# Second pass of a quantised feed-forward in written order, one PSUM bank per chunk; all keys in the first pass

## The chip, the cores and the metric

The kernel runs on one core of one Trainium2 chip. A core has a matrix engine (TensorE, PE in the profile; its weight loads are listed as PEld), a vector engine (VectorE, DVE), a scalar engine (ScalarE, ACT), a general engine (GpSimd, POOL) and a synchronising engine that issues transfers (SyncE, SP). Each engine works through its own instruction queue in order and waits there on semaphores that the others raise. Matrix products land in PSUM, which the kernel uses as eight banks of 2 KB a partition; a bank holds 512 fp32 values a partition. The metric is the time on the device in microseconds (us) of one execution of the whole program, lower is better.

## The reference, cut to what matters

Two transformer layers on an activation `x` of 16 x 256 x 256, each with a cross attention and a feed-forward. The change lies in the feed-forward of layer 0, which is quantised, and in what lies beside it: pieces of layer 1's attention that depend on the context alone.

```python
def quant_act_uint8(x):                       # one scale for the whole tensor
    s = max(max(x), EPS) / 255.0
    return clip(round(x / s), 0, 255) * s, s
def quant_linear(x, w, b):                    # weights int8 by channel, bias int32
    xq, s_in = quant_act_uint8(x)
    return einsum('btd,fd->btf', xq, wq) + bq
h = relu(quant_linear(layernorm(x), w1, b1))  # 256 -> 1024
x = x + quant_linear(h, w2, b2)               # 1024 -> 256
# layer 1 attention: correlation by delays of queries and keys, averaged over
# heads, channels and batch; the best 6 delays; softmax; values rolled by them
corr = irfft(rfft(q) * conj(rfft(k)))
index = top_k(corr.mean(...), 6)
```

The scale of `h` is a maximum over all of `h`, so no value of `h` can be quantised before the largest is known.

## The kernel before

The 4096 rows of `x` stay in SBUF as 32 tiles of 128 rows (`NT`), taken in 8 blocks (`NB`) of 4 tiles (`TB`), 512 rows each. The hidden width of 1024 is 8 chunks (`FC`) of 128, the model width of 256 is 2 (`DC`). A framework with tile pools builds the instruction streams: it puts in the semaphore waits, and where the code does not say otherwise, a scheduler chooses the order of instructions on each engine. Inside a `manual_schedule` region PE's instructions stand in the order in which the code writes them.

**First pass** (`first`, L914, and the loop from L1007). For each block, `integers_of` (L982) makes the block's integers: per tile one activation into a buffer `u` on ACT, two DVE operations, then 8 bf16 transposes into `qT`. For each pair of chunks, four matmuls (two chunks of two matmuls, 512 columns) fill a tile `ph` of two banks, and DVE reduces it to a maximum (`hmax`, L1013). PE's order is written out here. In the gaps stand keys of layer 1: `keys1` (L924) loads the context of one batch row (`ck`, on SP), turns it with four transposes, ACT writes `cT`, eight matmuls make `pk` and ACT writes `gT`. Four of the 16 keys are made ahead of the pass, ten in it, and the last two behind it in the scheduler's order.

**Max chain** (L1029 to L1051): DVE reduces `hmax`, POOL takes the maximum over partitions (`all_max`, L867), DVE works out the scale and the factors `a1`, `c1` of the next activation.

**Second pass** (loop at L1104 to L1112, scheduler's order). `hidden` (L1053) makes the same products again, a pair of chunks in a two-bank tile of the pool `ps_h` (two such tiles), ACT turns each chunk into `h32` (relu with scale and bias, L1060), DVE rounds it into `hq` (L1068). `second` (L1070) multiplies `hq` with the second weights (`py`, 16 matmuls a block), ACT writes `yT` (L1083), 8 transposes (`ytp`) turn it, DVE adds it to `x` (L1097) and takes the statistics of the next layer norm (`ln_stats`, L97), and once a block `ln_rstd` (L102) makes `rstd2` with eleven small DVE operations. The pools are `ps_h` (2 x 2 banks), `ps_b` (2) and `ps_y` (2): all eight banks.

**Start of layer 1's attention** (L1168 on, the x2 stage). `values1` (L957) is a product of context and value weights for one batch row, six matmuls on PE and a copy on ACT; it depends on nothing of layer 0 and fills PE where something is waited for. Three of them stand ahead of this stage. For each block, `ln_apply` (L118) makes normalised rows `xn`, eight transposes make `x2tp`, DVE and ACT copy them into `q`, and two groups of eight matmuls make `pm` (L1192) against `gT`; each `pm` goes through DRAM and comes back skewed (`skew`), and `diagonals` (L1142) adds them up in `pr`. Then `pmean` (L1248), with two `values1` ahead of the last diagonals and the rest, seven, behind `pmean`, while DVE and ACT find the best delays (L1254 to L1281), `cd` is written to DRAM and SP brings it back as `cm` (L1303); `po` (L1307) needs `cm`. Behind that stand the gates and a mixture of experts, which is most of the time.

Of the kernel before, what the change touches and what calls it, by code (L numbers as in the profile page):

```python
# [8 lines left out]
F32 = mybir.dt.float32  # L9
# [9 lines left out]
P = 128  # L19
# [9 lines left out]
def tile_kernel(ctx: ExitStack, tc: tile.TileContext, io: dict, out: bass.AP):  # L29
# [67 lines left out]
    def ln_stats(mv, t):  # L97
        st = small.tile([P, 6], F32, tag="bn", name=f"bn_{t}")
        nc.vector.bn_stats(st, x[:, t, :])
        nc.vector.bn_aggr(mv[:, t, :], st)  # L100

    def ln_rstd(rstd, mv, t0, n, who, by=1.0):  # L102

        ve = small.tile([P, n], F32, tag="ve", name=f"ve_{who}_{t0}")
        nc.vector.tensor_scalar(ve, mv[:, t0 : t0 + n, 1], LN_EPS, None, ALU.add)
        first = small.tile([P, n], I32, tag="r0", name=f"r0_{who}_{t0}")
        nc.vector.tensor_scalar(first, ve.bitcast(I32), -0.5, float(0x5F3759DF), ALU.mult, ALU.add)
        y = first.bitcast(F32)
# [771 lines left out]
    gq = until_keys.enter_context(tc.tile_pool(name="gq", bufs=1, side="right"))  # L880
    gT = gq.tile([P, B, DC, S], F32, name="gT")
    with tc.tile_pool(name="pb", bufs=2) as pb, tc.tile_pool(
        name="ps_h", bufs=2, space=PSUM
    ) as ps_h, tc.tile_pool(name="ps_b", bufs=2, space=PSUM) as ps_b, tc.tile_pool(
        name="ps_y", bufs=2, space=PSUM
    ) as ps_y:
        ln_rstd(rstd1, mv1, 0, NT, "1")
        g0 = sc.tile([P, NT], F32, name="g0")
        nc.vector.tensor_tensor(g0, rmax1, mv1[:, :, 0], ALU.subtract)
# [21 lines left out]
        qT = pb.tile([P, DC, NT * P], BF16, tag="qT", bufs=1, name="qT")  # L911
        hmax = sc.tile([P, FC, NB], F32, name="hmax")

        def first(blk, ph, fc):  # L914
            for c in range(DC):
                nc.tensor.matmul(  # L916
                    ph,
                    w1T[:, c, fc * P : (fc + 1) * P],
                    qT[:, c, blk * 512 : (blk + 1) * 512],
                    start=(c == 0),  # L920
                    stop=(c == DC - 1),
                )

        def keys1(b, pool=None, tag="y"):  # L924

# [77 lines left out]
        with tc.manual_schedule(engines={mybir.EngineType.PE}):  # L1003
            for _ in integers_of(0):
                pass
            key = None
            for blk in range(NB):  # L1007
                ahead = integers_of(blk + 1) if blk + 1 < NB else iter(())
                for f0 in range(0, FC, 2):
                    ph = ps_h.tile([P, 2, 512], F32, tag="h", name=f"ph1_{blk}_{f0}")  # L1010
                    for f in range(2):
                        first(blk, ph[:, f, :], f0 + f)
                    nc.vector.tensor_reduce(  # L1013
                        hmax[:, f0 : f0 + 2, blk], ph, axis=AX.X, op=ALU.max
                    )
                    if f0 < 4:
                        next(ahead, None)
                    if key is not None:
                        next(key)
                        key = None  # L1020
                    elif f0 == 2 or (f0 == 6 and blk % 4 == 0):
                        key = keys1(next(keyed))
                        next(key)
        for b in keyed:
            for _ in keys1(b):
                pass


        m1 = sc.tile([P, FC], F32, name="m1")  # L1029
# [20 lines left out]
        nc.vector.tensor_scalar(bq2, bq2, MAGIC, MAGIC, ALU.add, ALU.subtract)  # L1050
        nc.vector.tensor_mul(bq2, bq2, s2)  # L1051

        def hidden(blk, hq, f0):  # L1053

            ph = ps_h.tile([P, 2, 512], F32, tag="h", name=f"ph2_{blk}_{f0}")
            for f in range(2):
                fc = f0 + f
                first(blk, ph[:, f, :], fc)
                h32 = pb.tile([P, 512], F32, tag="h32", bufs=4, name=f"h32_{blk}_{fc}")
                nc.scalar.activation(  # L1060
                    h32,
                    ph[:, f, :],
                    AF.Relu,
                    bias=c1[:, fc : fc + 1],
                    scale=a1[:, fc : fc + 1],
                )

                nc.vector.tensor_scalar(hq[:, fc, :], h32, MAGIC, MAGIC, ALU.add, ALU.subtract)  # L1068

        def second(blk, hq):  # L1070

            yT = pb.tile([P, DC, 512], F32, tag="yT", name=f"yT{blk}")
            for c in range(DC):
                py = ps_y.tile([P, 512], F32, tag="y", name=f"py{blk}_{c}")
                for fc in range(FC):
                    nc.tensor.matmul(
                        py,
                        w2T[:, fc, c * P : (c + 1) * P],
                        hq[:, fc, :],
                        start=(fc == 0),  # L1080
                        stop=(fc == FC - 1),
                    )
                nc.scalar.activation(  # L1083
                    yT[:, c, :], py, AF.Identity, bias=bq2[:, c : c + 1], scale=s2[:, c : c + 1]
                )
                yield
            for i0 in range(0, TB, 2):
                t = blk * TB + i0
                tp = ps_b.tile([P, 2, D], F32, tag="b", name=f"ytp{blk}_{i0}")
                for i in range(2):  # L1090
                    for c in range(DC):
                        nc.tensor.transpose(
                            tp[:, i, c * P : (c + 1) * P],
                            yT[:, c, (i0 + i) * P : (i0 + i + 1) * P],
                            ident,
                        )
                nc.vector.tensor_tensor(x[:, t : t + 2, :], tp, x[:, t : t + 2, :], ALU.add)  # L1097
                for i in range(2):
                    ln_stats(mv2, t + i)
                if i0 + 2 == TB:  # L1100
                    ln_rstd(rstd2, mv2, blk * TB, TB, "2")
                yield

        pend = None  # L1104
        for blk in range(NB + 1):
            hq = pb.tile([P, FC, 512], BF16, tag="hq", name=f"hq{blk}") if blk < NB else None
            for f0 in range(0, FC, 2):
# [698 lines left out]
```

## Time and profile before

Times of three runs: 1407.86 us median, 1406.86 to 1409.86.

| what | value |
|---|---|
| profiled execution, its own time | 1407.56 us |
| its span, first to last instruction | 1405.9 us |
| mean granted clock of PE | 0.995 of full speed |
| PE busy in the span | 1358.8 us, 97% |
| DVE, ACT, POOL busy | 633.8, 553.3, 239.0 us |
| second pass, first relu to the last hq | 500.2 to 573.2 us |
| first `pm` of layer 1 | 581.70 us |

A row of the timeline gives the start, the busy time, the engine, the line of the kernel, the operation, what it writes and reads with the shapes, and how many in a row; in brackets the idle time before it and what ended it. Matmuls overlap, so the distance between two starts says more than the time of one.

### The profile page before, as it was taken

The page shows a single profiled execution, that of the slowest core. Times are in us where ns is not written, and L with a number is a line of the kernel's source. Part 1 is how long each engine was busy: PE and PEld are TensorE (multiplying, and loading weights), DVE is VectorE, ACT ScalarE, POOL GpSimd, SP SyncE. Part 2 cuts the span into 40 slices and gives each one's busy share as a digit, 9 for nine tenths or more (in the row PEclk, how much of TensorE's full clock was granted, in tenths as well). Part 3 has the DMA queues.
Part 4 walks back from the last instruction along what each step waited for, and adds up shares of the span by engine and source line. Part 5 has one row for each costly group of instructions (what it writes and reads, how often), then busy time and mean ns, then how long its engine had stood idle before and what let it go on. Part 6 is the DMA issues. An engine that isn't in the chain of part 4 may idle for free. (4 is left out here: it accounts for less than half of the span.)

```text
span 1405.9 us, 24030 instructions
## 1 busy us (share of the span) xinstructions
PE 1358.8 (97%) x8881; PEld 1035.8 (74%) x8955; DVE 633.8 (45%) x2520; ACT 553.3 (39%) x1050; POOL 239.0 (17%) x312
## 2 busy tenths in 40 slices
PE   6999999999989999999999999999999999999998
PEld 3565655666647644678788888888888888888887
DVE  7688879887737868857830101011011110101025
ACT  1454545554447568423622222323322323222221
POOL 6232133122000000000026530111111111111110
PEclk9899999999999999999999999999999999999999
DMA  9231323221001100333002245767666767665246
GB/s 276 78 96 54 105 85 91 70 73 27 17 18 37 45 0 1 112 98 96 3 31 83 72 156 195 249 231 244 244 248 233 246 236 257 234 232 190 96 155 220
DMA packets 127831, 184.06 MB, mean 131 GB/s; under 512 B 11600, under 2 KB 104952, under 8 KB 127712
## 3 DMA queue, kind: packets, MB, share of 16 engines
q1 hardware_dynamic: 117600, 152.55, 33.6%
q0 software_dynamic: 10112, 29.94, 6.1%
q8 instruction: 72, 1.18, 0.3%
q14 instruction: 47, 0.39, 0.1%
HBM read 141.16 MB, written 34.48 MB: 125 GB/s over the span
## 5 line engine op out<-in xcount | busy, mean ns | idle before, releaser
L1415 ACT ACTIVATE hTr<-pfr,bsel 128x256 f32<-128x256 f32 (+1 forms) x344 | 147.6, 430 | 345.9 <-PE pfr L1407 337.1
L1653 PE MATMUL ppr<-wp,hTr 128*128 128x256 f32 x1088 | 248.5, 379 | 0.0
L1407 PE MATMUL pfr<-xjT,wf 128*128 128x256 f32 (+1 forms) x1376 | 246.6, 338 | 0.7 <-DVE xjT L1643 0.7
L1407 PEld LDWEIGHTS pfr<-xjT,wf 128*128 128x128 f32 x1376 | 215.8, 191 | 30.3 <-issue 9.9
L1661 DVE TENSOR_TENSOR yj<-ppr,bj 128x512 f32<-128x512 f32 (+1 forms) x43 | 24.9, 580 | 440.3 <-PE ppr L1653 440.3
L1653 PEld LDWEIGHTS ppr<-wp,hTr 128*128 128x128 f32 x1088 | 202.1, 190 | 25.0
L511 DVE CUSTOM_DVE_ANT_0 junk<-sp,mb 128x256 bf16<-128x256 f32 x512 | 182.8, 420 | 37.6 <-PE sp L500 37.3
L588 ACT ACTIVATE pT<-st 128x1024 f32<-128x1024 f32 x128 | 124.4, 1021 | 125.9 <-PE st L578 125.9
L1679 POOL DMA_INDIRECT ys_d<-yj,to x68 | 65.4, 962 | 454.3 <-DVE to L1670 241.4
L1415 ACT ACTIVATE hTs<-pfs,bcol 128x256 f32<-128x256 f32 x128 | 59.9, 474 | 140.7 <-PE pfs L1407 137.5
L1407 PE MATMUL pfs<-xnT,wf-1_7251 128*128 128x256 f32 x512 | 114.5, 380 | 0.1
L1449 PE MATMUL pps<-wp-1_7253,hTs 128*128 128x256 f32 x496 | 109.6, 379 | 0.3 <-DVE x L1463 0.3
L1407 PEld LDWEIGHTS pfs<-xnT,wf-1_7251 128*128 128x128 f32 x512 | 96.4, 190 | 14.1 <-issue 1.4
L1449 PEld LDWEIGHTS pps<-wp-1_7253,hTs 128*128 128x128 f32 x496 | 94.2, 190 | 13.5 <-DVE x L1463 0.7
L500 PE MATMUL sp<-kT,qT 16*128 16x256 f32 x1024 | 93.4, 422 | 2.3 <-DVE mx L511 2.0
L568 PE MATMUL st<-qT,kT 32*128 32x256 f32 x1024 | 78.6, 404 | 0.7 <-DVE qT L549 0.7
L500 PEld LDWEIGHTS sp<-kT,qT 16*128 16x128 f32 x1024 | 59.2, 193 | 25.3 <-DVE mx L511 8.4
L1580 POOL DMA_INDIRECT xs_d<-xn,slot_i x64 | 61.8, 966 | 89.4 <-ACT hTs L1415 46.3
L601 PE MATMUL o<-pT,cxp 128*32 128x256 f32 x1024 | 73.6, 397 | 1.3 <-ACT pT L588 1.3
L916 PE MATMUL ph<-qT,w1T 128*128 128x512 bf16 x245 | 68.4, 378 | 4.0 <-DVE hmax L1013 1.4
L1463 DVE TENSOR_TENSOR x<-pps,x 128x512 f32<-128x512 f32 x15 | 10.4, 690 | 124.8 <-PE pps L1449 124.8
L568 PEld LDWEIGHTS st<-qT,kT 32*128 32x128 f32 x1024 | 50.7, 186 | 18.2 <-issue 12.4
(308 smaller groups left out, 1626.3 us busy)
## 6 DMA issues: line engine op xcount, KB each, us to landing
wf<-in_L_ffn_Wfc_dram SPq DMA_DIRECT2D x43, 1024.0 KB
wp<-in_L_ffn_Wproj_dram SPq DMA_DIRECT2D x43, 1024.0 KB, 5.7
xs_d<-zero POOLq DMA_DIRECT2D x36, 258.0 KB
yg<-ys_d SPq DMA_DIRECT2D x16, 512.0 KB, 6.4
xj<-xs_d SPq DMA_DIRECT2D x25, 258.0 KB
bj<-in_L_ffn_bproj_dram SPq DMA_DIRECT2D x43, 128.0 KB, 9.7
x<-in_x_dram SPq DMA_DIRECT2D x16, 256.0 KB, 10.7
cx<-in_ctx_dram SPq DMA_DIRECT2D x16, 256.0 KB, 2.7
```

The lines of the kernel that those rows point to most:

```text
L500: nc.tensor.matmul(sps[j // 2][:, j % 2, g, :], pr["qT"][rows, 2 * gp + g, qt * P : (qt + 1) * P], pr["kT"][rows, 2 * gp + g, :], start=Tr ...
L511: order["last"] = done = nc.vector.tensor_tensor_reduce(out=junk, in0=sps[j // 2][:, j % 2, g, :], in1=pr["mb"][:, qt, :], scale=1.0, scal ...
L568: nc.tensor.matmul(tps[j // 2][:, j % 2, k, :], pr["kT"][rows, g, k * P : (k + 1) * P], pr["qT"][rows, g, :], start=(k == 0), stop=False, ...
L588: nc.scalar.activation(pT, tps[i], AF.Exp)
L601: nc.tensor.matmul(pr["o"][HP * j : HP * (j + 1), g % 2, :], pr["cxp"][:, k, 4 * g + j, :], pTs[j // 2][:, j % 2, k, :], start=(k == 0), s ...
L916: nc.tensor.matmul(ph, w1T[:, c, fc * P : (fc + 1) * P], qT[:, c, blk * 512 : (blk + 1) * 512], start=(c == 0), stop=(c == DC - 1),)
L1407: nc.tensor.matmul(ph, wf[:, c, fc * P : (fc + 1) * P], rhs[:, c, :], start=(c == 0), stop=(c == DC - 1),)
L1415: nc.scalar.activation(hT[:, fc, :n], ph, AF.Gelu_apprx_tanh, bias=bias[:, fc : fc + 1]).ins
L1449: last = nc.tensor.matmul(po[:, i, :], hT[:, fc, i * P : (i + 1) * P], wp[:, fc, :], start=(fc == 0), stop=(fc == FC - 1),).ins
L1580: ins = nc.gpsimd.indirect_dma_start(out=xs_d, out_offset=bass.IndirectOffsetOnAxis(ap=slot_i[:, k, t : t + 1], axis=0), in_=xn3[t // QT][ ...
L1653: nc.tensor.matmul(po[:, i, :], hT[:, fc, i * P : (i + 1) * P], wp[:, fc, :], start=(fc == 0), stop=(fc == FC - 1),)
L1679: nc.gpsimd.indirect_dma_start(out=ys_d, out_offset=bass.IndirectOffsetOnAxis(ap=to[:, i : i + 1], axis=0), in_=yj[:, i, :], in_offset=None,)
```

## The change

Five things change together, all around the feed-forward of layer 0.

- The pools: `ps_y` and `ps_b` come first, `ps_h` is closed after the first pass, and its four banks become a pool `ps_k` of four tiles of one bank.
- The first pass: a key is begun in every second block at the last pair as well (before: in every fourth), so that all twelve keys are in the pass. Buffers of `u` go from 4 to 3. One `values1` follows the pass.
- The second pass is in written order on PE: per chunk its two first matmuls, two second matmuls of the block before, and one transpose of the block before that. Each chunk has a bank and a relu of its own; `first` names the previous relu as a dependency that takes part in the ordering alone and puts in no semaphore. A `values1` stands after chunk 3 of block 0 and another after the last second matmul.
- `rstd2` is made for blocks 0 to 3 together at block 3, for 4 to 6 at block 6, and for block 7 in the x2 stage; block 0's normalised rows (`xn_first`) are made at block 5.
- The x2 stage: one `values1` ahead of it instead of three, six instead of seven behind `pmean`; `ps_c` takes its banks after `ps_d` and `ps_r`.

```diff
     with tc.tile_pool(name="pb", bufs=2) as pb, tc.tile_pool(
-        name="ps_h", bufs=2, space=PSUM
-    ) as ps_h, tc.tile_pool(name="ps_b", bufs=2, space=PSUM) as ps_b, tc.tile_pool(
         name="ps_y", bufs=2, space=PSUM
-    ) as ps_y:
+    ) as ps_y, tc.tile_pool(name="ps_b", bufs=2, space=PSUM) as ps_b, ExitStack() as first_pass:
+        ps_h = first_pass.enter_context(tc.tile_pool(name="ps_h", bufs=2, space=PSUM))
...
-        def first(blk, ph, fc):
+        def first(blk, ph, fc, behind=None):
             for c in range(DC):
-                nc.tensor.matmul(
+                ins = nc.tensor.matmul(
...
+                if behind is not None and c == 0:
+                    tc.add_manual_dep(ins, behind.name, mybir.DependencyInfo(
+                            mybir.DependencyClass.NoSync, mybir.DependencyReason.DATA),
+                        reason="one chunk at a time")
...
-                u = pb.tile([P, D], F32, tag="u", bufs=4, name=f"u{t}")
+                u = pb.tile([P, D], F32, tag="u", bufs=3, name=f"u{t}")
...
-                    elif f0 == 2 or (f0 == 6 and blk % 4 == 0):
-                        key = keys1(next(keyed))
-                        next(key)
-        for b in keyed:
-            for _ in keys1(b):
-                pass
+                elif f0 == 2 or (f0 == 6 and blk % 2 == 0):
+                    key = keys1(next(keyed))
+                    next(key)
+        values1(next(valued), ps_b, "b")
+        first_pass.close()
+        ps_k = first_pass.enter_context(tc.tile_pool(name="ps_k", bufs=4, space=PSUM))
...
-        def hidden(blk, hq, f0):
-            ph = ps_h.tile([P, 2, 512], F32, tag="h", name=f"ph2_{blk}_{f0}")
-            for f in range(2):
-                fc = f0 + f
-                first(blk, ph[:, f, :], fc)
...
+        relus = []
+        def hidden(blk, hq, fc):
+            ph = ps_k.tile([P, 512], F32, tag="k", name=f"ph2_{blk}_{fc}")
+            first(blk, ph, fc, relus[-1] if relus else None)
+            h32 = pb.tile([P, 512], F32, tag="h32", bufs=4, name=f"h32_{blk}_{fc}")
+            relus.append(
                 nc.scalar.activation(
+                    h32, ph, AF.Relu, bias=c1[:, fc : fc + 1], scale=a1[:, fc : fc + 1]
+                ).ins
+            )
...
+                    if fc % 2 == 1:
+                        yield
...
-                if i0 + 2 == TB:
-                    ln_rstd(rstd2, mv2, blk * TB, TB, "2")
-                yield
+                            if i0 + 2 == TB and blk in (3, 6):
+                                b0 = 4 * (blk // 4)
+                                ln_rstd(rstd2, mv2, b0 * TB, (blk + 1 - b0) * TB, "2")
+                        yield
...
-        for blk in range(NB + 1):
-            hq = pb.tile([P, FC, 512], BF16, tag="hq", name=f"hq{blk}") if blk < NB else None
-            for f0 in range(0, FC, 2):
-                if blk < NB:
-                    hidden(blk, hq, f0)
-                if pend is not None:
-                    next(pend, None)
-            pend = second(blk, hq) if blk < NB else None
+        for blk in range(NB):
+            hq = pb.tile([P, FC, 512], BF16, tag="hq", name=f"hq{blk}")
+            for fc in range(FC):
+                hidden(blk, hq, fc)
+                next(mul, None)
+                next(turn, None)
+                if blk == 0 and fc == 3:
+                    values1(next(valued), ps_b, "b")
+            if blk == 5:
+                for i in range(TB):
+                    ln_apply(xn_first[:, i, :], mv2, rstd2, i)
+            turn = turned(blk - 1, yT) if blk > 0 else iter(())
+            yT = pb.tile([P, DC, 512], F32, tag="yT", name=f"yT{blk}")
+            mul = second(blk, hq, yT)
+        for _ in mul:
+            next(turn, None)
+        values1(next(valued), ps_b, "b")
+        for _ in turned(NB - 1, yT):
+            pass
...
-    ps_c = banks.enter_context(tc.tile_pool(name="ps_c", bufs=3, space=PSUM))
     ps_d = banks.enter_context(tc.tile_pool(name="ps_d", bufs=2, space=PSUM))
     ps_r = banks.enter_context(tc.tile_pool(name="ps_r", bufs=1, space=PSUM))
+    ps_c = banks.enter_context(tc.tile_pool(name="ps_c", bufs=3, space=PSUM))
...
-        for _ in range(3):
-            values1(next(valued), ps_c, "c")
+        values1(next(valued), ps_c, "c")
         for blk in range(NB):
-            xn = pc.tile([P, TB, D], F32, tag="xn", name=f"xn2_{blk}")
-            for i in range(TB):
-                ln_apply(xn[:, i, :], mv2, rstd2, blk * TB + i)
+            xn = xn_first
+            if blk > 0:
+                xn = pc.tile([P, TB, D], F32, tag="xn", name=f"xn2_{blk}")
+                for i in range(TB):
+                    ln_apply(xn[:, i, :], mv2, rstd2, blk * TB + i)
+            if blk == 1:
+                ln_rstd(rstd2, mv2, (NB - 1) * TB, TB, "2")
```

More of the change, by code (lines that the diff above doesn't have):

```diff
@@ L921, in first @@
                     stop=(c == DC - 1),
-                )
+                ).ins
+                if behind is not None and c == 0:
+                    tc.add_manual_dep(
+                        ins,
+                        behind.name,
+                        mybir.DependencyInfo(
+                            mybir.DependencyClass.NoSync, mybir.DependencyReason.DATA
+                        ),
+                        reason="one chunk at a time",
+                    )
         def keys1(b, pool=None, tag="y"):
@@ L999, in integers_of @@
                 yield
-        with tc.manual_schedule(engines={mybir.EngineType.PE}):
-            for _ in integers_of(0):
-                pass
-            key = None
-            for blk in range(NB):
-                ahead = integers_of(blk + 1) if blk + 1 < NB else iter(())
-                for f0 in range(0, FC, 2):
-                    ph = ps_h.tile([P, 2, 512], F32, tag="h", name=f"ph1_{blk}_{f0}")
-                    for f in range(2):
[L1012 to L1018, printed above, removed]
-                        next(key)
-                        key = None
-                    elif f0 == 2 or (f0 == 6 and blk % 4 == 0):
-                        key = keys1(next(keyed))
-                        next(key)
-        for b in keyed:
-            for _ in keys1(b):
-                pass
+        ordered = ExitStack()
+        ordered.enter_context(tc.manual_schedule(engines={mybir.EngineType.PE}))
+        for _ in integers_of(0):
+            pass
+        key = None
+        for blk in range(NB):
+            ahead = integers_of(blk + 1) if blk + 1 < NB else iter(())
+            for f0 in range(0, FC, 2):
+                ph = ps_h.tile([P, 2, 512], F32, tag="h", name=f"ph1_{blk}_{f0}")
+                for f in range(2):
+                    first(blk, ph[:, f, :], f0 + f)
+                nc.vector.tensor_reduce(
+                    hmax[:, f0 : f0 + 2, blk], ph, axis=AX.X, op=ALU.max
+                )
+                if f0 < 4:
+                    next(ahead, None)
+                if key is not None:
+                    next(key)
+                    key = None
+                elif f0 == 2 or (f0 == 6 and blk % 2 == 0):
+                    key = keys1(next(keyed))
+                    next(key)
+        values1(next(valued), ps_b, "b")
+        first_pass.close()
+        ps_k = first_pass.enter_context(tc.tile_pool(name="ps_k", bufs=4, space=PSUM))
         m1 = sc.tile([P, FC], F32, name="m1")
@@ L1051, in tile_kernel, with second @@
         nc.vector.tensor_mul(bq2, bq2, s2)
-        def hidden(blk, hq, f0):
-            ph = ps_h.tile([P, 2, 512], F32, tag="h", name=f"ph2_{blk}_{f0}")
-            for f in range(2):
-                fc = f0 + f
-                first(blk, ph[:, f, :], fc)
[L1059 to L1072, printed above, removed]
+        relus = []
[4 more added lines that the diff above has]
+            relus.append(
+                nc.scalar.activation(
+                    h32, ph, AF.Relu, bias=c1[:, fc : fc + 1], scale=a1[:, fc : fc + 1]
+                ).ins
+            )
+            nc.vector.tensor_scalar(hq[:, fc, :], h32, MAGIC, MAGIC, ALU.add, ALU.subtract)
+        def second(blk, hq, yT):
             for c in range(DC):
@@ L1082, in second, with turned @@
                     )
-                nc.scalar.activation(
-                    yT[:, c, :], py, AF.Identity, bias=bq2[:, c : c + 1], scale=s2[:, c : c + 1]
-                )
-                yield
+                    if fc == FC - 1:
+                        nc.scalar.activation(
+                            yT[:, c, :],
+                            py,
+                            AF.Identity,
+                            bias=bq2[:, c : c + 1],
+                            scale=s2[:, c : c + 1],
+                        )
+                    if fc % 2 == 1:
+                        yield
+        def turned(blk, yT):
             for i0 in range(0, TB, 2):
@@ L1096, in second @@
                         )
-                nc.vector.tensor_tensor(x[:, t : t + 2, :], tp, x[:, t : t + 2, :], ALU.add)
-                for i in range(2):
-                    ln_stats(mv2, t + i)
-                if i0 + 2 == TB:
-                    ln_rstd(rstd2, mv2, blk * TB, TB, "2")
-                yield
-        pend = None
-        for blk in range(NB + 1):
-            hq = pb.tile([P, FC, 512], BF16, tag="hq", name=f"hq{blk}") if blk < NB else None
-            for f0 in range(0, FC, 2):
-                if blk < NB:
-                    hidden(blk, hq, f0)
-                if pend is not None:
-                    next(pend, None)
-            pend = second(blk, hq) if blk < NB else None
+                        if i == 1 and c == DC - 1:
+                            nc.vector.tensor_tensor(
+                                x[:, t : t + 2, :], tp, x[:, t : t + 2, :], ALU.add
+                            )
+                            for j in range(2):
+                                ln_stats(mv2, t + j)
+                            if i0 + 2 == TB and blk in (3, 6):
+                                b0 = 4 * (blk // 4)
+                                ln_rstd(rstd2, mv2, b0 * TB, (blk + 1 - b0) * TB, "2")
+                        yield
+        mul, turn = iter(()), iter(())
+        xn_first = gq.tile([P, TB, D], F32, name="xn_first")
+        yT = None
+        for blk in range(NB):
+            hq = pb.tile([P, FC, 512], BF16, tag="hq", name=f"hq{blk}")
[15 more added lines that the diff above has]
+        for _ in turned(NB - 1, yT):
+            pass
+        ordered.close()
     sw = ctx.enter_context(tc.tile_pool(name="sw", bufs=1))
```

## The prediction

> **What bounds the kernel now.** I read the page's busy shares first, then the clock and the busy time of each engine by stage, then the start times inside the changed stage, then the chain behind the top-k. The page:
>
> ```profile
> span 1405.9 us, 24030 instructions
> PE 1358.8 (97%) x8881; PEld 1035.8 (74%) x8955; DVE 633.8 (45%) x2520; ACT 553.3 (39%) x1050; POOL 239.0 (17%) x312
> ```
>
> PE is the bound of the whole; a change pays only where PE stands idle. By stage (window, its length, PE, weight loads, DVE, ACT, POOL busy, granted clock, DMA share, GB/s):
>
> ```profile
> 440.00:502.00 62.00, 59.25 (x326) 38.87 (x333) 50.21 (x94) 39.01 (x111) 0.35 (x1) 1.00 0.13 39
> 502.00:573.00 71.00, 68.22 (x303) 30.11 (x307) 53.94 (x199) 55.76 (x79) 0.00 (x0) 1.00 0.00 1
> ```
>
> The first row is the first pass and the max chain, the second the second pass. Clock 1.00 in both. Busy PE is not PE at its peak: a lone matmul shows 0.38 us, but its successor can start earlier. The starts say what one costs. ScalarE (ACT) and PE in the second pass:
>
> ```profile
> 520.35 1.44 ACT L1060 ACTIVATE h<-ph,c,a 128x512 f32<-128x512 f32 x2
> ...
> 522.71 1.45 ACT L1060 ACTIVATE h<-ph,c,a 128x512 f32<-128x512 f32 x2 [0.24 <-PE ph L916]
> 524.83 1.45 ACT L1060 ACTIVATE h<-ph,c,a 128x512 f32<-128x512 f32 x2 [0.68 <-PE ph L916]
> 526.96 1.45 ACT L1060 ACTIVATE h<-ph,c,a 128x512 f32<-128x512 f32 x2 [0.68 <-PE ph L916]
> ...
> 529.34 1.44 ACT L1060 ACTIVATE h<-ph,c,a 128x512 f32<-128x512 f32 x2
> ```
> ```profile
> 568.94 0.38 PE L1076 MATMUL py<-hq,w2T 128*128 128x512 bf16 x1
> ...
> 569.61 1.46 PE L1076 MATMUL py<-hq,w2T 128*128 128x512 bf16 x6
> ...
> 574.72 0.38 PE L1092 MATMUL ytp<-ident,yT 128*128 128x128 f32 x2
> ...
> 575.37 0.82 PE L1092 MATMUL ytp<-ident,yT 128*128 128x128 f32 x6
> ```
>
> Six matmuls take 1.46, one 0.38: a pitch of (1.46-0.38)/5 = 0.216 us. Six transposes against two: (0.82-0.38)/4 = 0.11. A block of the second pass is 16 first matmuls, 16 second ones and 8 transposes: 32x0.2155+8x0.109 = 7.77 us. But ACT's first pair of a block starts at 520.35 and again at 529.34: the period is 8.99. Nor is ACT full: a second relu in a pair adds 0.67, so 8 relus and 2 yT are 10x0.67 = 6.7 (75%). What sets 8.99 is a loop. A pair of chunks shares one tile of two banks, and the instruction order has the pair's second chunk wait for ACT, that is for the first chunk's relu. So relu, matmuls, relu, matmuls follow each other, 2.13 us a pair (522.71, 524.83, 526.96), of which ACT waits 0.68.
>
> [...]
>
> The chain behind the top-k, where a cover gets shorter (PE, the transfer's issue on SP, PE):
>
> ```profile
> 627.07 0.70 PE L1248 MATMUL pmean<-r,avg 128*128 128x256 f32 x2 [0.73 <-DVE r L1246]
> ...
> 637.25 1.75 SPq L1303 DMA_DIRECT2D cm<-cd  x4
> ...
> 641.28 1.89 PE L1307 MATMUL po<-cT,cm 128*128 128x256 f32 x8
> ```
>
> and, of the sixteen cm transfers, from issue to landing:
>
> ```profile
> DMA to landing us min/median/max: 3.2/4.3/5.4
> ```
>
> From pmean to po PE is filled with seven values products.
>
> **The sum, as PE work and PE idle from the first pass (440.3) to the first pm (581.70).** Work before: 384 matmuls of 512 columns x0.2155 = 82.8; 64 ytp x0.109 = 7.0; 56 bf16 transposes x0.056 = 3.1; 12 keys x(4x0.109+8x0.2155 = 2.16) = 25.9; 3 values products x1.95 (starts 576.02, 577.00, 577.98) = 5.9; 8 x2tp 0.9. Together 125.5 of 141.4: idle 15.9. By start times 10.3 of it lies between 501.86 and 572.8 (8 blocks x1.2), 2.6 in the first pass, and 3 around the last two keys, the max chain and the q copies. After: the same work, and one values product more (four stand here): 127.5. The idle, part by part:
>
> - *First pass with all 12 keys.* The two keys move with all they issue (12 PE instructions each, their cT and gT writes on ACT, a ck load on SP each, which waits for one of three ck buffers and so leaves two keys ahead). PE then has 27.6+25.9+3.1 = 56.6, about 14.2 for two blocks, with DVE close behind: per block 4 hmax of 1.22 and 4 tiles of integers at 0.53 make 7.0, 14.0 for two. A block with one key is shorter on PE than on DVE, so PE waits for hmax there. Bounds: 0 (all averaged out) to 4 (before's 2.6 and half as much again; three u buffers for four count in it, as ACT has 23 of 62 us free). I take 1.6, nearest to the 2.6 seen. Pass ends 440.3+56.6+1.6 = 498.5.
> - *Max chain.* From the last hmax's start at 495.77 to c1's end at 499.09 it takes 3.3 us. PE now has one values product, four chunks in four fresh banks (1.7) and another product, 5.6 us in all: covered. Chunks 4-7 take 1.7 and run into the relus' rate of 0.67, about 0.25 of wait: block 0 ends at 506.1. Lower bound nothing; upper 1.4 if relus trail by two chunks.
> - *Blocks 1-7.* Each chunk has its own bank, so a chunk waits for the relu four chunks back, some 2.5 us of slack at 0.97 a chunk. The tie to the previous relu orders the scheduler's list but is no semaphore. ACT at 6.7 of 7.77 (86%) hides under PE. What is late next is DVE: 8 hq x0.34, 2 x-adds x0.6, 4 stats: 5.6; block 3 adds a 16-wide rstd (11 x0.2 = 2.2), block 6 a 12-wide one and the four rows for xn_first (1.4): 9.2 in a block of 7.77. The 1.5 over goes into four h32 buffers and four banks. Bounds 0 to 1.5; I take 0, as DVE has 2 us free in block 5 and 7. Block 1 is 6.9 (no transposes), six more 46.6, the last products and turns 4.3: 563.9.
> - *End.* From there PE has a values product, 8 ytp, another product, x2tp: 5.9 with two transposes of the next. DVE in that time: hq, x-adds, stats, xn of block 1, two q copies, one after another, about 8.05 to the first pm (before: 8.4 from the last py at 573.3 to 581.70, with three products inside). So PE idles 2.1; bounds 0 and 4.5 (if the 12-wide rstd falls in here too). First pm 571.95: **-9.75**.
> - *x2 stage.* The rstd of block 7 stands in DVE's queue ahead of block 1's q copy; 11 ops of 0.2 against 4.9 us a pm block: +0.2 (0 to 2.2).
> - *After pmean.* Six products cover instead of seven: PE would be free at 627.07+0.5+11.7 = 639.3 on before's clock, and the first cm, issued at 637.25, lands 3.2 to 5.4 later; it was there at 641.07, when the first weights for po loaded. So it landed between 640.45 and 641.07: a new wait of 1.2 to 1.8 against 1.95 saved: -0.15 (-0.75 to -0.1). SP's issue depends on the top-k chain alone.
>
> Everything behind is PE-bound (14.00 us with 13.93 busy from 627 to 641; 39.00 of 39.00 to 680) and moves along. Sum -9.75+0.2-0.15 = **-9.7**. The profiled execution took 1407.56 (span 1405.9 and 1.66 around it), 0.3 below the median 1407.86: **1397.9**.
>
> **Rivals.** About 0.2% (2.8 us) is what a measurement of this kernel can tell from no change.
>
> 1. *The end gives part back.* The loop goes, but its gain runs into DVE: 1.5 in block 6, 4.5 instead of 2.1 at the end, 2.2 in the x2 stage: +1.5+2.4+2.0 = 5.9, a gain of 3.8: 1403.8. For it: xn, stats and q copies stand in one DVE queue, which shows no idle between 577.1 and 582. Against it: DVE works 54 of 71 us in the second pass, and the x2 stage has 25.7 of 45.
> 2. *Other side: the written order stalls PE.* A matmul that waits now holds everything behind it in PE's queue, where before the scheduler had chosen what was ready. The place is the second products: they wait for hq on DVE, which waits for relu, which waits for a chunk in that same PE queue. It decides when a block takes longer than 8.99+ (3 saved elsewhere)/7 = 9.4; if each chunk waited a full round (chunk 0.43, relu 0.78, ACT's 0.68 less the 0.43 of matmuls in it) the block would be 8x1.46 = 11.7, 7x(11.7-8.99) = +19 less 3: 1423. Against it: the products use the block before, whose last hq is due 1.2 us after its relu's start (0.78+0.43) while the order puts that product 3 chunks (2.9 us) later. Half the mechanism (a block of 9.4) gives no change.
> 3. *Clock.* The lowest granted digit on the page is 8; the second pass's 62 us at 0.8 instead of 1.00 cost 15.5: 1413. The windows above stand against it: four banks in turn already, with waits in each pair, at 1.00. [...]
>
> **Numbers.** Forecast case (gain 6 to 14: at best all 3.95 of idle left in the sum goes, at worst half of the upper ends come together) 0.70; rival 1 0.14; rival 2 0.12, of which 0.04 within 0.2%; rival 3 0.02; nothing changed in effect 0.02. Faster 0.82 (0.70, and 0.12 of rival 1), same 0.08, slower 0.10. The range is from 1394 (4 better) to 1404.5 (rival 1 taken in); outside lie rivals 2 and 3.
>
> **What would show it.** Right: relu pairs without the 0.68 wait, a block period of 7.8 on PE, the first pass ending near 498.5, the first pm near 572, a wait of 1.2 to 1.8 before the first po. Wrong: a period over 9, PE waits on hq or relu in every chunk, idle over 4 before the first pm, or a clock under 1.00 in the pass.

## The result, and the profile after

The changed kernel takes 1396.07 us (median of four, 1394.68 to 1397.19), the kernel before 1407.36 beside it; the ratio is 0.9927 with a 95% interval of 0.9909 to 0.9945. Forecast were 1397.9 and a range of 1394 to 1404.5. The profiled execution took 1397.19, 10.4 us less than that of before.

The page of the changed kernel, its busy shares:

```profile
span 1395.4 us, 24082 instructions
PE 1361.9 (98%) x8955; PEld 1038.6 (74%) x8955; DVE 625.7 (45%) x2465; ACT 552.9 (40%) x1050; POOL 238.5 (17%) x312
```

PE's busy time is 3 us more (74 of its matmul records were missing before), the span 10.5 less. By stage, the columns as before; the second row is the second pass, the third a stretch in its middle:

```profile
440.00:500.00 60.00, 59.15 (x335) 39.45 (x335) 47.86 (x80) 39.28 (x111) 0.00 (x0) 1.00 0.14 40
500.00:564.00 64.00, 63.90 (x325) 34.49 (x324) 48.84 (x157) 56.56 (x81) 0.35 (x1) 1.00 0.00 1
515.00:556.00 41.00, 41.00 (x213) 22.45 (x212) 33.51 (x108) 37.82 (x55) 0.00 (x0) 1.00 0.01 1
```

PE is busy in 41.00 of 41.00 us. (Before, the pass showed 68.22 of 71.00 by this measure, though a seventh of each block, 1.22 of 8.99, lay open between the starts.) ACT in the second pass:

```profile
522.06 2.35 ACT L1073 ACTIVATE h<-ph,c,a 128x512 f32<-128x512 f32 x3
524.61 0.78 ACT L1073 ACTIVATE h<-ph,c,a 128x512 f32<-128x512 f32 x1 [0.20 <-PE ph L917]
525.29 0.77 ACT L1093 ACTIVATE yT<-py,bq,s 128x512 f32<-128x512 f32 x1
525.95 2.35 ACT L1073 ACTIVATE h<-ph,c,a 128x512 f32<-128x512 f32 x3
...
529.84 1.45 ACT L1073 ACTIVATE h<-ph,c,a 128x512 f32<-128x512 f32 x2
```

From 522.06 to 529.84 eight relus and two yT: a block takes 7.78 us, 8.99 before. The wait of 0.68 in each pair has become 0.20 ahead of every fourth relu: ACT now waits for PE's own pace. PE, one chunk, two second matmuls, one transpose:

```profile
523.01 0.59 PE L917 MATMUL ph<-qT,w1T 128*128 128x512 bf16 x2
523.44 0.59 PE L1085 MATMUL py<-hq,w2T 128*128 128x512 bf16 x2
523.87 0.27 PE L1110 MATMUL ytp<-ident,yT 128*128 128x128 f32 x1
523.98 0.59 PE L917 MATMUL ph<-qT,w1T 128*128 128x512 bf16 x2
```

The starts are 0.97 apart by chunk (523.01, 523.98), 4x0.2155+0.109, so nothing is left between them. What PE still waits for from here to po stands at the end of the pass, ahead of pmean and before po:

```profile
567.33 0.66 PE L1110 MATMUL ytp<-ident,yT 128*128 128x128 f32 x4 [0.24 <-ACT cT L980]
568.79 0.27 PE L971 MATMUL pv<-bvo,ones 65*128 65x256 bf16 x1 [0.81 <-DVE x L1116]
...
572.34 0.92 PE L1234 MATMUL pm<-q,gT 128*128 128x256 f32 x3 [0.16 <-DVE q L1224]
...
618.00 0.70 PE L1290 MATMUL pmean<-r,avg 128*128 128x256 f32 x2 [0.73 <-DVE r L1288]
...
631.89 0.45 PE L1349 MATMUL po<-cT,cm 128*128 128x256 f32 x1 [1.47 <-DMA cm<-cd]
```

Laid beside the trace of before by equal instructions, PE's instructions are 9.3 us earlier from the first po to 1390 us, without change. The other 1.1 us of the profile's gain comes in the last 30 us, where the last gathers (yg) come back from DRAM and PE waits for the additions behind them: 0.32 and 1.32 us before, once 0.71 after. On the chain that ended last, five of the gathers took 28.1 us before and 23.7 after. The change doesn't touch them, and the kernels below show how far they scatter.

### The profile page after: what moved, and what is told of

The parts are those of the page before. It is cut to its first block, busy times and chain, and to the rows that moved or that the text cites. A ratio compares the mean times of both kernels' runs of the same rounds, so it can differ in the third digit from the quotient of the medians.

```text
span 1395.4 us, 24082 instructions
## 1 busy us (share of the span) xinstructions
PE 1361.9 (98%) x8955; PEld 1038.6 (74%) x8955; DVE 625.7 (45%) x2465; ACT 552.9 (40%) x1050; POOL 238.5 (17%) x312
## 5 line engine op out<-in xcount | busy, mean ns | idle before, releaser
L578 PE MATMUL st<-mbT,ident 128*128 128x512 bf16 x256 | 67.2, 385 | 0.0
L1505 DVE TENSOR_TENSOR x<-pps,x 128x512 f32<-128x512 f32 x15 | 10.4, 690 | 125.2 <-PE pps L1491 125.2
```

The lines of the kernel that those rows point to most:

```text
L578: nc.tensor.matmul(tps[i][:, j].rearrange("p k q -> p (k q)"), ident16, pr["mbT"].rearrange("p k q -> p (k q)"), start=False, stop=True, s ...
```

## The experiments

The whole time scatters by several us between executions of one kernel (1402.61 to 1409.14 for the kernel before, in one series of sixteen). In the profiled executions of all the kernels the first `ph` starts between 437.54 and 441.71, and from the first `po` to the end they take 762.8 to 768.3; the changes lie between the two. So each kernel is read by a stretch of its own trace as well: from the first matmul of the first pass (`ph`) to the first `po`. Before it is 641.28-440.19 = 201.09 us, after 631.89-439.93 = 191.96. A block is the distance of eight relus in the middle of the second pass.

| kernel | ratio to before, 95% | ph to po | against before | block |
|---|---|---|---|---|
| before | | 201.09 | | 8.99 |
| the change | 0.9927 (0.9909 to 0.9945) | 191.96 | -9.1 | 7.78 |
| changed_again | 0.9937 (0.9914 to 0.996) | 191.69 | -9.4 | 7.78 |
| banks_only | 0.994 (0.9924 to 0.9957) | 193.59 | -7.5 | 7.89 |
| free_order | 0.9953 (0.9937 to 0.9969) | 191.93 | -9.2 | 7.78 |
| two_single | 0.9978 (0.9963 to 0.9994) | 194.98 | -6.1 | 7.78 |
| two_banks | 1.0118 (1.0091 to 1.0144) | 216.47 | +15.4 | 10.46 |
| one_bank | 1.0223 (1.0195 to 1.025) | 229.98 | +28.9 | 11.68 |
| keys_only | 1.0019 (1.0002 to 1.0035) | 203.33 | +2.2 | 8.99 |
| keys_back | 0.9961 (0.9942 to 0.9981) | 194.26 | -6.8 | 7.78 |
| rstd_each | 0.9937 (0.9917 to 0.9957) | 192.28 | -8.8 | 7.78 |
| lean_end | 0.9939 (0.9918 to 0.996) | 191.76 | -9.3 | 7.78 |
| lean_tail | 0.992 (0.9904 to 0.9937) | 190.53 | -10.6 | 7.78 |
| best | 0.9947 (0.9924 to 0.9969) | 191.39 | -9.7 | 7.78 |

The first is a yardstick, the changed kernel itself, run beside others.

> The changed kernel once more, as the yardstick for the runs beside it: ratio to the kernel before 0.9927 within its interval, 0.991 to 0.9945. Both theories alike.

It came out so, and the stretch repeats within 0.3 us, where the medians of the two series differ by 1.1.

### What the bank for each chunk does

**One part alone: banks_only.** The kernel before, with this, the relu reading `ph`, and the four single banks that it takes (the pools `ps_y`, `ps_b`, `ps_h` and `ps_k` as in the change), and nothing else:

```diff
-            ph = ps_h.tile([P, 2, 512], F32, tag="h", name=f"ph2_{blk}_{f0}")
             for f in range(2):
                 fc = f0 + f
-                first(blk, ph[:, f, :], fc)
+                ph = ps_k.tile([P, 512], F32, tag="k", name=f"ph2_{blk}_{fc}")
+                first(blk, ph, fc)
```

> The kernel before with one thing changed: in the second pass each chunk has a single bank of its own, four of them (pools as in the changed kernel). Order by the scheduler, keys, values products, rstd and the rest as before. Theory A (the shared tile alone makes the 8.99 us period): block period 7.8 to 8.1, 7 to 9 us faster than before, ratio 0.9935 to 0.995. Theory B (the package is needed: order, tie, values products placed for cover): 4 us or less, 0.997 and up.

Measured -7.5 in the stretch, ratio 0.994: theory A. The block is 7.89 with the scheduler's own order, which runs eight second matmuls in a row between pairs of chunks. PE of banks_only:

```profile
518.85 1.89 PE L1077 MATMUL py<-hq,w2T 128*128 128x512 bf16 x8
520.57 1.03 PE L915 MATMUL ph<-qT,w1T 128*128 128x512 bf16 x4
521.44 1.89 PE L1077 MATMUL py<-hq,w2T 128*128 128x512 bf16 x8
523.16 1.03 PE L915 MATMUL ph<-qT,w1T 128*128 128x512 bf16 x4
```

Eight second matmuls take 1.72 from start to start, two chunks 0.87, which is 0.215 and 0.218 for each matmul: in these rows nothing waits, and the second chunk of a pair no longer waits for the relu on the first. It was the tile of two banks that carried the wait, not the banks.

So the tiles alone bring 7.5 of the 9.1 us. The remaining 1.6 are the other parts together.

**The order left to the scheduler: free_order.** The changed kernel, with the written order ended before the second pass:

```diff
+        ordered.close()
         first_pass.close()
...
         for _ in turned(NB - 1, yT):
             pass
-        ordered.close()
```

> The changed kernel with its banks and its chunk by chunk code, but the scheduler chooses PE's order in the second pass (the written order ends with the first pass). Theory A (the banks bring the gain, the order is secondary): block period 7.8 to 8.1, within 3 us of the changed kernel. Theory B (the written order brings it): period near 9, 1403 or more.

The stretch is the same to 0.03 us, the block to 0.01. With a bank for each chunk, and with the tie to the previous relu in its list, the scheduler arrives at the written order in the middle of the pass: two first matmuls, two second ones, one transpose. Writing the order out brings nothing of itself. (banks_only, without the tie, has another order and a block of 7.89.)

**The written order without the banks: two_banks.**

```diff
-        ps_k = first_pass.enter_context(tc.tile_pool(name="ps_k", bufs=4, space=PSUM))
+        ps_k = first_pass.enter_context(tc.tile_pool(name="ps_k", bufs=2, space=PSUM))
...
-            ph = ps_k.tile([P, 512], F32, tag="k", name=f"ph2_{blk}_{fc}")
+            if fc % 2 == 0:
+                pair.append(ps_k.tile([P, 2, 512], F32, tag="k", name=f"ph2_{blk}_{fc}"))
+            ph = pair[-1][:, fc % 2, :]
```

> The changed kernel, but the chunks of the second pass share two-bank tiles again, two chunks a tile; the written order stays. Theory A (the shared tile makes the loop relu, chunk, relu): the second chunk of a pair may start only when the first one's relu is done, 0.59 of matmuls + 0.04 + 0.78 of relu + 0.05 = 1.46 us after the first's start, where the order has it 0.97 later. A pair takes 1.46+0.97 = 2.43, a block 9.7 instead of 7.8, eight blocks +14: about 1410, slower even than the kernel before. Theory B (the written, finer interleaving is what brings the gain, the bank for each chunk does little): within 3 us of the changed kernel, below 1400.

Slower than the kernel before by 15.4 us, and by 24.5 than the changed one, not by the 14 expected. The sign of theory A holds, its size does not. PE of two_banks:

```profile
521.15 0.27 PE L1113 MATMUL ytp<-ident,yT 128*128 128x128 f32 x1
522.23 0.59 PE L917 MATMUL ph<-qT,w1T 128*128 128x512 bf16 x2 [0.80 <-ACT h L1076]
...
523.09 0.27 PE L1113 MATMUL ytp<-ident,yT 128*128 128x128 f32 x1
523.20 0.59 PE L917 MATMUL ph<-qT,w1T 128*128 128x512 bf16 x2
...
524.66 0.59 PE L917 MATMUL ph<-qT,w1T 128*128 128x512 bf16 x2 [0.33 <-ACT h L1076]
```

and its ACT:

```profile
520.06 0.78 ACT L1076 ACTIVATE h<-ph,c,a 128x512 f32<-128x512 f32 x1 [0.68 <-PE ph L917]
520.74 0.77 ACT L1096 ACTIVATE yT<-py,bq,s 128x512 f32<-128x512 f32 x1
521.40 0.78 ACT L1076 ACTIVATE h<-ph,c,a 128x512 f32<-128x512 f32 x1
522.86 0.78 ACT L1076 ACTIVATE h<-ph,c,a 128x512 f32<-128x512 f32 x1 [0.68 <-PE ph L917]
```

The round of 1.46 is there (523.20 to 524.66). What I had left out is the yT: it stands between two relus in ACT's queue, so the second chunk waits for relu, yT and relu (0.80 here and 0.69 later in the block, instead of 0.33). By the starts further on in the trace a pair with a yT takes 2.79 (525.63 to 528.42), a pair without 2.43 (523.20 to 525.63) as worked out; two of each make the block of 10.46 against 9.7. The scheduler of before had avoided a part of this with the same tiles: it put only one second matmul between the second chunk of a pair and the first of the next, left the others to the wait, and came to 8.99.

**Fewer single banks: one_bank and two_single.** The only edit is the number of tiles in `ps_k`:

```diff
-        ps_k = first_pass.enter_context(tc.tile_pool(name="ps_k", bufs=4, space=PSUM))
+        ps_k = first_pass.enter_context(tc.tile_pool(name="ps_k", bufs=1, space=PSUM))
```

> The changed kernel with one single bank for the chunks instead of four: a chunk waits for the relu just before it, as it would if the ordering tie were a real wait. Theory A: 1.46 us a chunk, a block 11.7, eight blocks +31: about 1427. Rival: ACT is fed in any case and the products of the block before fill the wait, +5 or less.

> The changed kernel with two single banks instead of four. Theory A (what counts is that a chunk does not wait for the relu of its neighbour): a round of 1.46 fits into two pitches of 0.97, only a yT between two relus (0.67) makes it 2.13 against 1.94, 0.2 twice a block: +0.4 a block; and behind the max chain only two chunks can go ahead, +1.4. Together +1.5 to +4.5: 1397.5 to 1400.5. Rival (four banks of slack are needed against the jitter of ACT and DVE): +8 or more.

One bank: a block of 11.68 = 8x1.46, as worked out; the whole is +38 against the changed kernel where +31 was expected, the 7 more lying in the first two blocks, before the products fill the waits, where the clock falls as well (14.58 and 12.10 instead of 5.79 and 6.63; the clock in the last section). Two banks: 7.78, not the 0.4 more that I had put to each block, so one yT between two relus still fits; but +3.0 over the first three blocks (7.54, 7.59, 7.67 against 5.79, 6.63, 7.27), where +1.4 was expected. The other two of the four banks serve the start alone: four chunks go ahead while the scale is not there yet.

### What the keys do

**keys_only** is the kernel before with `blk % 2` in the key condition, **keys_back** the changed kernel with `blk % 4`, the two keys behind the pass and the values product of that place ahead of the x2 stage:

```diff
-                elif f0 == 2 or (f0 == 6 and blk % 2 == 0):
+                elif f0 == 2 or (f0 == 6 and blk % 4 == 0):
...
-        values1(next(valued), ps_b, "b")
+        for b in keyed:
+            for _ in keys1(b):
+                pass
         first_pass.close()
...
-        values1(next(valued), ps_c, "c")
+        for _ in range(2):
+            values1(next(valued), ps_c, "c")
```

> The kernel before with the key condition changed alone: all twelve keys in the first pass, nothing else. The pass becomes 4.3 us longer by two keys that are gone behind it, and the 3.3 us of the max chain lose their cover save for four chunks (1.7). Theory: -1 to +1 us, no gain of its own. Rival (keys fill the pass's waits for hmax, and the max chain costs nothing): -2 or more.

> The changed kernel with ten keys in the first pass again and the last two written behind it, in place of the values product there, which goes ahead of the x2 stage. Theory: the pass has fewer keys to fill DVE's 7.0 us a block, so PE waits more there, +0.5 to +2 against the changed kernel. Rival: the keys' place does not matter, within 0.3 us of the shift in the trace.

Both missed by little, and on the same side. keys_only loses 2.2 us. PE of keys_only at the max chain, the third row of relus on ACT, and four-microsecond windows:

```profile
498.20 1.46 PE L916 MATMUL ph<-qT,w1T 128*128 128x512 bf16 x5
500.54 0.59 PE L916 MATMUL ph<-qT,w1T 128*128 128x512 bf16 x2 [0.89 <-DVE hmax L1013]
503.50 0.59 PE L916 MATMUL ph<-qT,w1T 128*128 128x512 bf16 x2 [2.36 <-ACT h L1060]
...
507.28 1.45 ACT L1060 ACTIVATE h<-ph,c,a 128x512 f32<-128x512 f32 x2 [1.71 <-PE ph L916]
```
```profile
502.00:506.00 4.00, 2.50 (x7) 0.84 (x7) 2.37 (x11) 2.22 (x3) 0.00 (x0) 0.74 0.00 0
506.00:510.00 4.00, 3.91 (x14) 1.40 (x13) 0.89 (x3) 2.03 (x3) 0.00 (x0) 0.83 0.00 0
```

PE stands still for 0.89 and 2.36 us, and then the granted clock is 0.74 and 0.83 for eight microseconds: 2.50x0.26+3.91x0.17 = 1.3 us more on the matmuls in them, an estimate. About 1.0 of it reaches ACT, which waits 1.71 there where other pairs of this pass wait about 0.69. But the loss itself stands ahead of that: the first relu comes 62.36 us after the first ph instead of 60.02, with the max chain uncovered. The block behind it takes 9.56 against 9.66, because before the late keys' work on ACT held up the second relu there by about as much (502.79 after 500.21). In keys_back the two keys wait for their own cT (0.56 and 0.86, PE at 496.98 and 500.27), and at the last second matmul it is 0.7 behind the changed kernel; the values product that makes room for the keys costs its full 1.9 ahead of the x2 stage, and 0.3 comes back behind that: +2.3. So, as far as these two kernels show, moving the keys is worth something only because values products take their place behind the pass, and they do that without waiting for anything.

### The end of the pass

**rstd_each** makes rstd2 once a block again; **lean_end** keeps the twelve-wide chain out of the end:

```diff
-                            if i0 + 2 == TB and blk in (3, 6):
+                            if i0 + 2 == TB and blk in (3, 4):
...
-                ln_rstd(rstd2, mv2, (NB - 1) * TB, TB, "2")
+                ln_rstd(rstd2, mv2, 5 * TB, 3 * TB, "2")
```

(rstd_each has `if i0 + 2 == TB: ln_rstd(rstd2, mv2, blk * TB, TB, "2")` at that place and no chain in the x2 stage.)

> The changed kernel with rstd2 once a block again (four tiles wide, eleven operations of about 0.2 us each time) instead of three times in all; xn_first stays. DVE then has 5.6+2.2 = 7.8 us in every block of 7.8, and block 7's chain falls into the end of the pass. Theory: the passes keep 7.8 thanks to the buffers, the end grows by up to 2.2: +0.5 to +3 in the trace behind the pass. Rival (DVE's small operations hide anyway): within 0.3.

> The changed kernel with the second rstd made at block 4 (for block 4 alone) and the third in the x2 stage for blocks 5 to 7, so that the twelve-wide chain of 2.2 us, seen between 566.5 and 570.3 in the end of the pass, is gone from there. Theory (DVE's queue sets the first pm): first pm 1 to 1.7 us earlier. Rival (PE's own work and the x-add set it): 0.3 or less.

rstd_each: +0.3, the rival. Eleven small operations in every block cost next to nothing in this trace. lean_end: the first pm comes 132.30 us after the first ph instead of 132.41, the rival again. The chain of 2.2 us is gone from DVE there, and PE still stands:

```profile
566.93 0.69 DVE L1116 TENSOR_TENSOR x<-ytp,x 128x512 f32<-128x512 f32 x1 [0.70 <-PE ytp L1110]
567.13 0.66 PE L1110 MATMUL ytp<-ident,yT 128*128 128x128 f32 x4 [0.24 <-ACT cT L980]
567.83 0.69 DVE L1116 TENSOR_TENSOR x<-ytp,x 128x512 f32<-128x512 f32 x1 [0.20 <-PE ytp L1110]
...
568.57 0.27 PE L971 MATMUL pv<-bvo,ones 65*128 65x256 bf16 x1 [0.78 <-DVE x L1116]
```

DVE itself waits now (0.70, 0.20). What comes late are the transposes: they stand behind a whole values product, their second half waits until that product's bank is copied out (0.24), and the next product waits for the x-add of that half (0.78). So **lean_tail** writes the transposes between the product's two halves, and gives it a bank of `ps_y` (`values1` runs the generator that it is handed after its third matmul):

```diff
-        values1(next(valued), ps_b, "b")
-        for _ in turned(NB - 1, yT):
-            pass
+        values1(next(valued), ps_y, "y", turned(NB - 1, yT))
```

> lean_end, and the last eight transposes are written between the two halves of the values product behind the last second matmul (in a bank of the other pool), not behind the whole of it, so they start about 1 us earlier, just as yT is ready. Theory: first pm another 0.5 to 1 us earlier than lean_end, in all 1.5 to 2.5 earlier than the changed kernel: 1394 to 1395 beside 1396.5. Rival: the wait moves to the q copies, no gain over lean_end.

PE of lean_tail:

```profile
564.60 1.03 PE L973 MATMUL pv<-wvo,cT 128*128 128x256 f32 x4
565.47 1.04 PE L1113 MATMUL ytp<-ident,yT 128*128 128x128 f32 x8
566.34 0.27 PE L971 MATMUL pv<-bvo,ones 65*128 65x256 bf16 x1
...
571.00 0.70 PE L1235 MATMUL pm<-q,gT 128*128 128x256 f32 x2
```

All eight transposes run in a row, 1 us earlier, and the first pm stands 131.11 us behind the first ph, 1.2 earlier than in lean_end. That is a little more than was expected over lean_end, and less than the 1.5 to 2.5 over the changed kernel, because lean_end had brought next to nothing. Whether the place of the transposes or the other bank does it was not parted. In the stretch lean_tail is 1.4 us ahead of the changed kernel, the best of all. Its median, 1396.19 beside 1406.45, and its ratio of 0.992 (0.9904 to 0.9937) can't be told from the changed kernel's, and in its profiled execution the five gathers on the last chain took 3 us more than in the changed kernel's.

**best** adds one thing to it, to take away the wait for cm: no values product after chunk 3 of block 0, and so seven behind pmean.

```diff
-                if blk == 0 and fc == 3:
-                    values1(next(valued), ps_b, "b")
```

> lean_tail, and the values product after chunk 3 of block 0 is left out there, so that seven instead of six stand behind pmean. At the max chain PE then has 3.7 us of cover for 3.4 and the next chunks run at the relus' 0.67: 1.2 us more idle there, 1.6 of wait for cm less. Theory: 0.2 to 0.5 earlier than lean_tail at the first po. Rival (the cover at the max chain was needed in full): 1 or more later.

The start behaves about as worked out (0.76 of wait before the fifth chunk, then 0.24 for each of four), the first pm comes 130.64 us after the first ph, 0.5 earlier than in lean_tail, and cm no longer holds po. But:

```profile
629.23 0.59 ACT L983 COPY cT<-pv 128x512 f32<-128x512 f32 x1 [1.37 <-PE pv L973]
...
629.87 1.35 PE L1348 MATMUL po<-cT,cm 128*128 128x256 f32 x5 [0.68 <-ACT cT L983]
```

po now waits for ACT's copy of the seventh product, 0.68 us. By the stretch po comes 0.9 later than in lean_tail, which is the size of the rival but not its reason: leaving out the product at the max chain saved more than the new waits there cost. Before, po started ahead of the copy of the seventh product (641.28 and 641.48). The code suggests why this can happen: with `ps_c` allocated behind `ps_d` and `ps_r`, its banks are the ones that po's pool gets later, which they were not before. That is argued from the order of the pools alone and was not tried; a kernel with the old order of the three pools and seven products stays open.

## Why the prediction was right, step by step

- *The loop.* The block was to take 7.77 and takes 7.78; ACT's 86% hides. banks_only shows the cause: the shared tile, and 7.5 of the 9.1 us with it.
- *First pass.* Its last matmuls start at 497.89 and end with the next product's start at 498.75; 498.5 was worked out; counted from the first ph, which came 0.4 earlier than taken, that is 0.6 late. Three waits of 0.39 for hmax and some at the start make 1.9 of idle, 1.6 was taken.
- *Max chain.* One wait of 0.24, at 506.36 (start to start); 0.25 was taken.
- *Blocks 1-7.* The last second matmul gives way at 564.53; 563.9 was worked out, so 1.0 late counted from the first ph. DVE's 1.5 too much in block 6 went into the buffers, as taken.
- *End.* From there 7.8 to the first pm, 8.05 was worked out, with 1.7 of idle (0.40, 0.98 and 0.32 start to start) for 2.1. Size right, cause half right: the step had DVE's queue alone, full from the last products on, set the first pm. lean_end shows that the twelve-wide chain in that queue costs 0.1, and that DVE waits 0.70 and 0.20 for the transposes, which stand behind a values product and wait for the bank that it hands on. Only from the last x-add on does DVE's queue show no idle up to the q copies: 4.28 us to the first pm in the changed kernel, 4.20 in lean_end, 4.17 in lean_tail. The agreement in size is luck in part.
- *x2 stage.* From pm to pmean 45.66 against 45.37: +0.3, with +0.2 taken.
- *After pmean.* The wait is 1.47 in the row, 1.2 to 1.8 was worked out; pmean to po is 13.89 against 14.21, -0.3 with -0.15 taken.
- *Sum.* The first pm is 9.36 earlier (9.75), the first po 9.39; 0.26 of that was there at the first ph, so that 9.1 are the stage's own. The remaining 1 us of the profile lies in the last gathers, of which the prediction said nothing. The medians are 11.3 apart in the first series and 9.7 in changed_again's; what goes beyond the 9.1 can't be given to the change, and that the second comes out at the 9.7 forecast is luck.

Of the rivals, the first had the end for the wrong reason, and next to nothing of its 5.9 came (0.1 in the x2 stage). The second, the other side, is a real mechanism: in two_banks, written order holds up PE in the way described, the block passes the 9.4 from which it was to decide (10.46), and the kernel loses 15.4. It did not come because no chunk waits for its neighbour's relu any more; the prediction gave its place wrongly as the second matmuls, it is the chunk itself. The third did not come: the clock was granted at 1.00 through the pass (500 to 564 us), with four banks in turn and PE busy in 41.00 of 41.00 us in its middle; two_banks, with PE waits of 0.33 and 0.69 in turn, has 1.00 from 502 to 582 us as well. A chunk of four matmuls and a transpose takes 0.97 us, which leaves 0.215 for each matmul, and ACT waits 0.20 ahead of every fourth relu: PE, not ACT, is the floor of the pass.

## What to carry to other kernels

A tile that spans two banks is one tile to whoever puts in the waits (a block of 8.99 us with it, 7.89 in banks_only): give each piece that has its own reader a tile of its own before anything is reordered. A written order is worth what its waits allow; the same order gains 9 us with single banks and loses 15 with shared ones, and the scheduler found the order unasked once the tiles were right and each chunk was tied to the relu before it. Put work that waits for nothing where a chain must be covered, and look, when a cover is moved, which bank its last piece hands on to the next.

## What the runs showed of the hardware, unexpected

The clock fell after waits of 0.87 to 2.36 us in two of the kernels, one_bank and keys_only. In one_bank, four-microsecond windows of its first block, and sixty microseconds of its later ones:

```profile
502.00:506.00 4.00, 2.12 (x7) 0.76 (x7) 1.28 (x3) 1.65 (x3) 0.00 (x0) 0.85 0.00 0
506.00:510.00 4.00, 3.56 (x13) 2.41 (x12) 0.43 (x1) 1.55 (x3) 0.00 (x0) 0.72 0.00 0
...
514.00:518.00 4.00, 3.12 (x9) 1.00 (x8) 0.85 (x2) 1.78 (x3) 0.00 (x0) 0.63 0.00 0
...
530.00:590.00 60.00, 46.48 (x205) 21.64 (x205) 34.48 (x106) 38.74 (x52) 0.00 (x0) 1.00 0.00 1
```

In the first block PE is busy for 0.59 us of every 1.46, and the clock goes to 0.63 at worst, with 1.00 from 510 to 514 between; later, with second matmuls in the wait, it is busy for three quarters of the time and the clock is 1.00. In keys_only one wait of 2.36 us behind one of 0.89 was followed by 0.74 and 0.83; in two_single one of 1.46 was not (1.00 in its windows from 498 to 514), nor in two_banks one of 1.88 and three of 0.98 to 1.10, with 0.9 to 2.8 us of matmuls between them (1.00 in the same windows). No run shows what tells these cases from the falls. The max chain, uncovered, cost more than its wait in keys_only, by about 1.0 us on ACT's relus.
